# A two-layer graph network on one core: loads in order of use, and two slots of the main loop in another order

## The chip, the cores and the metric

The kernel runs on one core of a Trainium2 chip. The core has five engines that work side by side and wait for each other through semaphores: TensorE (matrix products, and the loading of weights for them), VectorE, ScalarE, GpSimd and SyncE (which issues most of the transfers). The metric is the device time of one execution in microseconds (us), as the median of several runs. In the profile TensorE's products are PE and its weight loads PEld, VectorE is DVE, ScalarE is ACT, GpSimd is POOL, and the queue of SyncE is SPq.

## What is computed

`x` is 64 graphs of 256 nodes with 512 features in float32; `adj` is one 256 x 256 matrix of zeros and ones that all of them share. Layer 0 is a graph convolution, layer 1 an attention of 8 heads under the mask of `adj`. After each, the input is added and the rows are normalized.

```python
# layer 0
Wi, Wj = W[:, :512], W[:, 512:]
mi, mj = x @ Wi.T, x @ Wj.T                       # per graph: 256x512 @ 512x512
out = deg[:, None] * (mi + b) + a @ mj            # a = adj as float, deg = its row sums
x = layernorm(x + out)
# layer 1
q, k, v = (split_heads(x @ W.T + b) for W, b in ((Wq, bq), (Wk, bk), (Wv, bv)))   # 8 heads of 64
scores = where(adj == 0, -inf, q @ k.T / 8)
out = merge_heads(softmax(scores) @ v) @ Wo.T + bo
x = layernorm(x + out)
```

## The kernel before

Every 512 x 512 product is made of seven products of half blocks in place of eight, Strassen's scheme in Winograd's form: sums of blocks of the left operand (`S1` to `S4`, made on VectorE) meet sums of blocks of the weights (`T1` to `T4`, made once). The kernel's list of layer-0 steps for one graph `b` is this (steps 1 to 7 are the seven products, each of four records on TensorE; `bank` gives one of three PSUM banks, `score_banks` one of two pairs of banks):

```python
def left_steps(f, order=anywhere):
    return [lambda: order(nc.vector.tensor_add(f["S1"], f["A21"], f["A22"])),   # L477
            lambda: order(nc.vector.tensor_sub(f["S2"], f["S1"], f["A11"])),   # L478
            lambda: order(nc.vector.tensor_sub(f["S3"], f["A11"], f["A21"])),  # L479
            lambda: order(nc.vector.tensor_sub(f["S4"], f["A12"], f["S2"]))]   # L480
# ... (cut)
    def split(t):
        nc.scalar.copy(k["hi"][:, t, :], k["mj"][:, t, :])                      # L524
        nc.gpsimd.tensor_tensor(k["lo"][:, t, :], k["mj"][:, t, :],             # L525
                                k["hi"][:, t, :].bitcast(F32), ALU.subtract)

    def step1():
        product("x", raw(0, 0), B11, True)
        nc.scalar.copy(keeper("u1"), banks["x"])
    def step2():
        product("w", raw(1, 1), T4, True)
        add_scaled(1, banks["w"])
    def step3():
        product("x", raw(0, 1), B21, False)
        add_scaled(0, banks["x"])
    def step4():
        product("y", xS[b]["S2"], T2, True)
        nc.vector.tensor_add(keeper("u2"), banks["y"], k["u1"])
    def step5():
        product("z", xS[b]["S1"], T1, True)
        k["mj"] = p1.tile([P, NT, D], F32, tag="mj", name="mj")
        nc.scalar.copy(k["mj"][:, 1, :], banks["z"])                            # L547
    def step6():
        product("y", xS[b]["S3"], T3, False)
        nc.vector.tensor_add(keeper("u3"), banks["y"], k["u1"])                 # L551
        nc.gpsimd.tensor_tensor(k["mj"][:, 1, :], k["mj"][:, 1, :], k["u3"], ALU.add)   # L552
        # ... (cut: tiles for hi and lo)
        split(1)
        add_scaled(1, k["u3"])                                                  # L520
    def step7():
        product("z", xS[b]["S4"], B22, False)
        nc.vector.tensor_add(k["mj"][:, 0, :], banks["z"], k["u2"])             # L561
        split(0)

    def neighbours():                       # the graph's product, a @ mj, in two parts of mj
        k["pa"] = score_banks("pa")
        for i in (1, 0):
            for n, (j, part) in enumerate((j, part) for j in (1, 0) for part in ("hi", "lo")):
                matmul(k["pa"][:, i, :], graph[:, j, i * P:(i + 1) * P], k[part][:, j, :],
                       start=(n == 0), stop=(n == 2 * NT - 1))
    def take(t):                            # adds pa to xh, statistics of the normalization
    def give(t):                            # normalizes; send_h writes the result out, turned
    return [step1, step2, step3, step4, step5, step6, step7, neighbours, lambda: take(1), lambda: take(0),
            lambda: give(1), lambda: send_h(b, 1), lambda: give(0), lambda: send_h(b, 0)]
```

Attention goes by units `w` of two heads of one graph. `scores` starts the score products and returns the rest, which adds the mask on VectorE, takes the exponential on ScalarE and adds up on GpSimd:

```python
def scores(g, w):
    ps = score_banks("ps").rearrange("p j (t q) -> p j t q", t=NT)
    # ... (cut: eight score matmuls into ps)
    def exponentials():
        pe = p2.tile([P, 2, NT, N], F32, tag="pe", name="pe")
        nc.vector.tensor_add(pe, ps, maskT)                                     # L805, operands cut
        in_order(nc.scalar.activation(flat, flat, AF.Exp, scale=QSCALE, ...))   # L809
        nc.gpsimd.tensor_tensor(pk, pe[:, :, 0, :], pe[:, :, 1, :], ALU.add)    # L812
    return exponentials
```

The main loop makes 31 passes. In each, the attention of two graphs is mixed with layer 0 of the next two (`p` and `q` are their lists of steps), slot by slot:

```python
def layer0(g):
    p, q = l0_steps(b1), l0_steps(b2)
    return [p[:3] + [item(turn_x, b2)] + p[3:4],
            p[4:7] + [item(sum_x, b2), item(add_bias, b2)] + q[:1],
            p[7:10], p[10:] + q[1:3],
            q[3:6] + [item(turn_h, b1)] + q[6:7],
            q[7:], [item(turn_h, b2)]]
# ... (cut)
for g in range(NG - 1):
    # ... (cut)
    run(work[0])
    for w in range(2, NB * NC, 2):          # w = 2, 4, 6: the second, third and fourth slot
        values(g, w - 2)                    # products with v, into pav
        values(g, w - 1)
        multiply()                          # aoT times the spread inverses of the slot before, GpSimd (L844)
        divide_two(g, w - 1)                # den on TensorE, reciprocal on VectorE (L887), spread by transfers
        scores(g, w)()
        if w == 4:
            run(work[2])
        later = scores(g, w + 1)
        later()
        run(work[w // 2 if w < 4 else w // 2 + 1])
```

`turn_x(b)` transposes the loaded `x` on VectorE (L485), `sum_x(b)` makes its four sums (`xS`), `add_bias(b)` adds the bias times the degrees to `xh` on GpSimd (L374). In the opening, `make_factors` makes `T1` to `T4` of an attention weight with four VectorE subtractions and writes them to memory, and `check_graph` makes the mask with three VectorE operations.

Of the kernel before, what the change touches and what calls it, by code (L numbers as in the profile page):

```python
# [8 lines left out]
F32 = mybir.dt.float32  # L9
# [7 lines left out]
P = 128  # L17
# [207 lines left out]
def unshifted_path(ctx, tc, flag, x, adj, wiT, wjT, b0, wqT, bq, wkT, bk, wvT, bv, woT, bo, out):  # L225
# [72 lines left out]
    def load_x(b):  # L298
        if b < B:
            xh[b] = p6.tile([P, NT, D], F32, tag="xh", name="xh")  # L300
            nc.sync.dma_start(out=xh[b], in_=x[b].rearrange("(t p) d -> p t d", p=P))
# [1 line left out]
    b_bc = p4.tile([P, D], F32, tag="u", name="b_bc")  # L303
    xB, hB = {}, {}

    def load_xB(b):
        if b < B:
            xB[b] = p1.tile([P, N // R, P], F32, tag="xB", name="xB")
            for q in range(D // P):
                nc.sync.dma_start(out=xB[b][q * R:(q + 1) * R],  # L310
                                  in_=x[b][:, q * P:(q + 1) * P].rearrange("(r a) n -> r a n", r=R))
# [1 line left out]
    load_xB(0)  # L313
    w0 = const.tile([P, 7, 2, D], F32, name="w0")
    adj_i = p2.tile([P, NT, N], I32, tag="pe", name="adj_i")
    for n, w, h in ((B11, wiT, 0), (T3, wjT, 0), (None, None, 0), (B21, wiT, 1), (B22, wjT, 1)):
        if n is None:
            nc.sync.dma_start(out=adj_i, in_=adj.rearrange("(t p) j -> p t j", p=P))
        else:
            nc.sync.dma_start(out=w0[:, n], in_=w.rearrange("(p h c) o -> p h c o", h=2, c=2)[:, h])  # L320
    load_x(0)
    nc.sync.dma_start(out=b_bc, in_=b0.to_broadcast([P, D]))

    xT, xS, hT, hS, qT, kT, vv, aoT, oS = ({} for _ in range(9))
# [44 lines left out]
    def degree_bias():  # L369
        for t in range(NT):  # L370
            in_order(nc.vector.tensor_scalar(degb[:, t, :], b_bc, deg[:, t:t + 1], None, ALU.mult))
# [116 lines left out]
    def turn_x(b, tag="xT"):  # L488
        if b < B:
            xT[b] = p1.tile([P, NC, N], F32, tag=tag, name="xT")  # L490
            transposed(xT[b], xB.pop(b))
            load_xB(b + 1)

    def sum_x(b):
        if b < B:
# [6 lines left out]
    def l0_steps(b):  # L502
        banks, k = {}, {}

        def product(name, left, n, first):
            if first:
                banks[name] = bank("po")
            for c in range(2):
                matmul(banks[name], left[:, c, :], w0[:, n, c, :], start=(first and c == 0),
                                 stop=(c == 1), skip_group_check=True)  # L510

        def raw(t, h):
            return xT[b][:, 2 * h:2 * h + 2, t * P:(t + 1) * P]

        def keeper(name):
            k[name] = p3.tile([P, D], F32, tag="lu", name=name)
            return k[name]

        def add_scaled(t, src):
            nc.vector.scalar_tensor_tensor(xh[b][:, t, :], src, deg[:, t:t + 1], xh[b][:, t, :],  # L520
                                           ALU.mult, ALU.add)

        def split(t):
            nc.scalar.copy(k["hi"][:, t, :], k["mj"][:, t, :])  # L524
            nc.gpsimd.tensor_tensor(k["lo"][:, t, :], k["mj"][:, t, :], k["hi"][:, t, :].bitcast(F32),  # L525
                                    ALU.subtract)
# [14 lines that stand above are left out]
            product("y", xS[b]["S2"], T2, True)  # L541
            nc.vector.tensor_add(keeper("u2"), banks["y"], k["u1"])

        def step5():
            product("z", xS[b]["S1"], T1, True)
            k["mj"] = p1.tile([P, NT, D], F32, tag="mj", name="mj")
            nc.scalar.copy(k["mj"][:, 1, :], banks["z"])  # L547

        def step6():
            product("y", xS[b]["S3"], T3, False)  # L550
            nc.vector.tensor_add(keeper("u3"), banks["y"], k["u1"])  # L551
            nc.gpsimd.tensor_tensor(k["mj"][:, 1, :], k["mj"][:, 1, :], k["u3"], ALU.add)  # L552

            k["hi"] = p1.tile([P, NT, D], F32R, tag="hi", name="hi")
            k["lo"] = p1.tile([P, NT, D], F32R, tag="lo", name="lo")
            split(1)
            add_scaled(1, k["u3"])

        def step7():
# [4 lines that stand above are left out]
        stats = {}  # L564

        def neighbours():
# [6 lines that stand above are left out]
        def take(t):  # L573
            r = xh[b][:, t, :]
            in_order(nc.vector.tensor_add(r, k["pa"][:, t, :], r))
            stats[t] = norm_stats(r, in_order)

        def give(t):
            norm_apply(xh[b][:, t, :], *stats[t], in_order)


        return [step1, step2, step3, step4, step5, step6, step7, neighbours, lambda: take(1), lambda: take(0),
                lambda: give(1), lambda: send_h(b, 1), lambda: give(0), lambda: send_h(b, 0)]

# [315 lines left out]
    def layer0(g):  # L900

        b1, b2 = NB * g, NB * g + 1

        def item(f, *args):
            return lambda: f(*args)

        p, q = l0_steps(b1), l0_steps(b2)
        return [p[:3] + [item(turn_x, b2)] + p[3:4],
                p[4:7] + [item(sum_x, b2), item(add_bias, b2)] + q[:1],
                p[7:10], p[10:] + q[1:3],  # L910
                q[3:6] + [item(turn_h, b1)] + q[6:7],
                q[7:], [item(turn_h, b2)]]

    def run(steps):
        for s in steps:
            s()

    def with_output_bias(g, k):
        return [*k[:2], lambda: add_output_bias(NB * g), k[2], lambda: add_output_bias(NB * g + 1), *k[3:]]
# [8 lines left out]
    def combine(n, m, k):  # L928
        in_order(nc.vector.tensor_sub(w0[:, n], w0[:, m], w0[:, k]))
# [11 lines left out]
    combine(T2, B22, T1)  # L941
    combine(T4, B21, T2)
    combine(T3, B22, T3)
    p, q = l0_steps(0), l0_steps(1)
    run([p[0], p[2], p[4], p[3]])
    turn_x(1, "hB")
    degree_bias()
    add_bias(0)
    turn_graph()
    run([p[1], p[5], q[0], p[6], q[2]])  # L950
# [22 lines left out]
    h_transpose(1, 1)  # L973
    h_transpose(1, 0)
    run(o[2:])
    check_graph()
    run(with_output_bias(0, k)[2:])
    run(v[2:3])
    turn_x(2)
    sum_x(2)  # L980
    add_bias(2)
    run(v[3:5])
    make_factors(woT, "wo", raw_o)
    load_x(3)
    run([scores(0, 0), scores(0, 1)])
    run(v[5:])
    for g in range(NG - 1):
        load_x(NB * (g + 2))
        load_x(NB * (g + 2) + 1)
        work = layer0(g + 1)  # L990
        run(work[0])
        for w in range(2, NB * NC, 2):
            values(g, w - 2)
            values(g, w - 1)
            multiply()
            divide_two(g, w - 1)
            scores(g, w)()
            if w == 4:
                run(work[2])
            later = scores(g, w + 1)  # L1000
            later()
            run(work[w // 2 if w < 4 else w // 2 + 1])
        w = NB * NC - 2
        values(g, w)
        values(g, w + 1)
        multiply()
        o = o_steps(g)
        q = second_late(qk_steps(g + 1, qT, "qT", bq_sb, bqd))
        k = second_late(qk_steps(g + 1, kT, "kT", bk_sb, bkd, True))
        v = second_late(v_steps(g + 1, True))  # L1010
        neighbours, take1, take0, give1, send1, give0, send0 = work[SLOTS + 1]
        inverses = divide_at_once(g, w + 1, lambda: run([o[0], neighbours, take1, take0]))
        run([q[0], give1, send1, o[1], give0, send0, *left_steps(oS[g], in_order), k[0], q[1], k[1]])
        end_values(inverses)
        run(o[2:6] + work[SLOTS + 2] + [v[0], o[6], v[1]])
        end = finish_steps(g)
        k = with_output_bias(g + 1, k)[2:]
        run(q[2:5] + end[:1] + q[5:6] + end[1:2] + q[6:7] + end[2:3] + k[:1] + end[3:4] + k[1:] + end[4:] + v[2:3])
        turn_x(NB * (g + 2))
        sum_x(NB * (g + 2))  # L1020
        if g + 2 < NG:
            add_bias(NB * (g + 2))
        run(v[3:5])
        run([scores(g + 1, 0), scores(g + 1, 1)])
        run(v[5:])
# [93 lines left out]
```

## Time and profile before

| | |
|---|---|
| time, median of 3 runs | 3117.78 us (3116.93 to 3118.83) |
| span of the profiled execution | 3115.8 us |
| VectorE busy | 2227.6 us, 71% |
| GpSimd busy | 1504.5 us, 48% |
| ScalarE busy | 998.4 us, 32% |
| transfers | 439.13 MB, 141 GB/s on average |
| mean granted clock of TensorE | 0.999 |

A row of a timeline reads: start in us from the span's beginning, duration in us, engine, source line, operation, output and inputs by name, shape, count of instructions that were merged; in square brackets the idle time of the engine ahead of it and what ended it. A busy share is an average over the whole span. An engine that is idle elsewhere can still be the one that is waited for in one slot, so the rows of the slots matter more here than the shares.

### The profile page before, as it was taken

The numbers are of one execution on the slowest core, as the hardware profiler recorded it, in microseconds if no ns is written. First come the engines' busy times: TensorE is split into PE (matmuls) and PEld (weight loads), VectorE is DVE, ScalarE is ACT, GpSimd is POOL, SyncE is SP. The second block draws the span as 40 slices with busy tenths as digits, with TensorE's granted clock in tenths as the row PEclk, the third lists the DMA queues.
The fourth block names the chain that finished last, engine by engine and source line by source line (L and its number), as shares of the span: only waits on it lengthen the run. The fifth ranks groups of instructions, "written<-read, shape, count | busy, mean of one in ns | idle before, by whom it ended". The sixth has DMA issues, their size and how long they took to land. (4 is left out here: it accounts for less than half of the span.)

```text
span 3115.8 us, 42525 instructions
## 1 busy us (share of the span) xinstructions
PE 3082.4 (99%) x14598; PEld 2131.7 (68%) x14598; DVE 2227.6 (71%) x3327; ACT 998.4 (32%) x1894; POOL 1504.5 (48%) x1255
## 2 busy tenths in 40 slices
PE   8999999999999999999999999999999999999998
PEld 4667766677766777666776667776677766677665
DVE  6777777776777767776777777677776777767775
ACT  2332333323333333333233332333333333323332
POOL 2544445544545445454454544454544546445453
PEclk9999999999999999999999999999999999999999
DMA  7345534455444554445553445544455444555332
GB/s 252 118 146 153 162 116 131 129 154 160 139 119 125 152 164 144 117 129 149 154 162 113 132 132 153 162 134 121 125 152 166 142 117 127 151 157 159 111 112 93
DMA packets 398490, 439.13 MB, mean 141 GB/s; under 512 B 36928, under 2 KB 288320, under 8 KB 397888
## 3 DMA queue, kind: packets, MB, share of 16 engines
q1 hardware_dynamic: 398272, 436.36, 46.7%
q8 instruction: 120, 1.97, 0.3%
q14 instruction: 98, 0.80, 0.1%
HBM read 340.79 MB, written 70.25 MB: 132 GB/s over the span
## 5 line engine op out<-in xcount | busy, mean ns | idle before, releaser
L461 POOL TENSOR_TENSOR rstd<-ve,mhalf 128x1 f32<-128x1 f32 x256 | 140.4, 552 | 717.7 <-DVE below L459 717.7
L812 POOL TENSOR_TENSOR pk<-pe 128x512 f32<-128x512 f32 x256 | 322.1, 1274 | 336.4 <-ACT pe L809 336.2
L290 PE MATMUL po<-w,xS 128*128 128x512 f32 x1024 | 471.7, 603 | 6.1 <-ACT mj L547 5.7
L290 PE MATMUL st<-hS,factor 128*128 128x256 f32 x2048 | 452.7, 379 | 1.2 <-DVE u L685 1.2
L290 PEld LDWEIGHTS st<-hS,factor 128*128 128x128 f32 x2048 | 388.4, 190 | 55.1 <-DVE u L685 1.6
L809 ACT ACTIVATE pe<-pe 128x1024 f32<-128x1024 f32 x256 | 270.8, 1058 | 379.2 <-DVE pe L805 379.2
L290 PE MATMUL po<-w,xT 128*128 128x512 f32 x768 | 354.0, 603 | 12.9 <-DVE xT L485 10.9
L290 PEld LDWEIGHTS po<-w,xS 128*128 128x128 f32 x1024 | 187.5, 190 | 253.5 <-issue 192.6
L290 PE MATMUL st<-hT,factor 128*128 128x256 f32 x1536 | 360.1, 381 | 0.7 <-ACT hT L622 0.7
L290 PEld LDWEIGHTS st<-hT,factor 128*128 128x128 f32 x1536 | 289.0, 190 | 52.4 <-ACT u L711 11.8
L805 DVE TENSOR_TENSOR pe<-ps,maskT 128x1024 f32<-128x1024 f32 x256 | 297.9, 1194 | 32.9 <-PE ps L290 32.9
L290 PEld LDWEIGHTS po<-w,xT 128*128 128x128 f32 x768 | 144.1, 191 | 181.0 <-issue 163.3
L290 PE MATMUL ps<-qT,kT 64*128 64x256 f32 x2048 | 264.9, 392 | 0.0
L290 PE MATMUL pav<-pe,v_sb 128*64 128x256 f32 x2048 | 250.1, 386 | 1.9 <-ACT pe L809 1.8
L740 DVE TENSOR_TENSOR xh<-st,xh 128x512 f32<-128x512 f32 x186 | 142.9, 768 | 138.1 <-PE st L290 138.1
L290 PEld LDWEIGHTS pav<-pe,v_sb 128*64 128x64 f32 x2048 | 135.2, 136 | 154.2 <-issue 71.9
L290 PEld LDWEIGHTS ps<-qT,kT 64*128 64x128 f32 x2048 | 184.3, 186 | 78.2 <-issue 51.3
L290 PE MATMUL st<-factor,hS 128*128 128x256 f32 x1024 | 234.8, 382 | 0.0
L888 POOL TENSOR_TENSOR rtot<-rtot,rden 128x256 f32<-128x256 f32 x96 | 70.0, 729 | 332.2 <-DVE rden L887 332.2
L290 PE MATMUL st<-factor,oS 128*128 128x256 f32 x992 | 224.2, 379 | 0.0
L887 DVE RECIPROCAL rden<-den 128x256 f32<-128x256 f32 x96 | 168.4, 1754 | 71.6 <-PE den L290 70.0
L290 PEld LDWEIGHTS st<-factor,hS 128*128 128x128 f32 x1024 | 191.9, 190 | 35.4 <-issue 10.6
(115 smaller groups left out, 4808.1 us busy)
## 6 DMA issues: line engine op xcount, KB each, us to landing
xB<-in_x_dram SPq DMA_DIRECT2D x256, 128.0 KB, 3.6
xh<-in_x_dram SPq DMA_DIRECT2D x64, 512.0 KB, 4.1
factor<-wq SPq DMA_DIRECT2D x128, 256.0 KB, 3.6
factor<-wk SPq DMA_DIRECT2D x128, 256.0 KB, 2.6
factor<-wv SPq DMA_DIRECT2D x128, 256.0 KB, 2.6
factor<-wo SPq DMA_DIRECT2D x124, 256.0 KB, 2.9
h_cols<-xh SPq DMA_DIRECT2D x124, 256.0 KB, 2.4
hB<-h_cols SPq DMA_DIRECT2D x62, 512.0 KB, 3.6
```

What stands on the lines that cost most here:

```text
L290: in_order(nc.tensor.matmul(*args, **kw))
L461: nc.gpsimd.tensor_tensor(rstd, ve, mhalf, ALU.pow)
L740: nc.vector.tensor_add(dst, src, dst)
L805: nc.vector.tensor_add(pe.rearrange("p j t q -> p j (t q)"), ps.rearrange("p j t q -> p j (t q)"), maskT.rearrange("p t q -> p (t q)").uns ...
L809: in_order(nc.scalar.activation(flat, flat, AF.Exp, scale=QSCALE, accum_out=etot[:, NB * g + i, pr:pr + 1]))
L812: nc.gpsimd.tensor_tensor(pk, pe[:, :, 0, :], pe[:, :, 1, :], ALU.add)
L887: nc.vector.reciprocal(rden, den)
L888: nc.gpsimd.tensor_tensor(rtot, rtot, rden, ALU.add)
```

## The change

It has four parts. In the opening, the weights' loads stand in the order in which they are used and the first goes through ScalarE's queue, and the second `x` is loaded early into a buffer of its own and transposed earlier. Further on in the opening, the factors of `wo` are made earlier and the graph's check later. In the second slot the products come as step 6, step 5, the next graph's step 1, step 7, so that more work lies between step 5 and step 7, which share a bank; `join` lets step 5 and 6 come in either order. In the third slot both groups of scores come together, then a product of the next graph, then the graph's product, then another product.

```diff
-    def load_xB(b):
+    def load_xB(b, tag="xB"):
...
-    for n, w, h in ((B11, wiT, 0), (T3, wjT, 0), (None, None, 0), (B21, wiT, 1), (B22, wjT, 1)):
-        if n is None:
-            nc.sync.dma_start(out=adj_i, in_=adj.rearrange("(t p) j -> p t j", p=P))
-        else:
-            nc.sync.dma_start(out=w0[:, n], in_=w.rearrange("(p h c) o -> p h c o", h=2, c=2)[:, h])
+    for queue, n, w, h in ((nc.scalar, B11, wiT, 0), (nc.sync, B21, wiT, 1), (nc.sync, T3, wjT, 0), (nc.sync, B22, wjT, 1)):
+        queue.dma_start(out=w0[:, n], in_=w.rearrange("(p h c) o -> p h c o", h=2, c=2)[:, h])
+    nc.sync.dma_start(out=adj_i, in_=adj.rearrange("(t p) j -> p t j", p=P))
     load_x(0)
+    load_xB(1, "hS")
...
-            load_xB(b + 1)
+            if b > 0:
+                load_xB(b + 1)
...
+        def join(*needed):
+            if all(n in k for n in needed):
+                nc.gpsimd.tensor_tensor(k["mj"][:, 1, :], k["mj"][:, 1, :], k["u3"], ALU.add)
+                k["hi"] = p1.tile([P, NT, D], F32R, tag="hi", name="hi")
+                k["lo"] = p1.tile([P, NT, D], F32R, tag="lo", name="lo")
+                split(1)
...
-                p[4:7] + [item(sum_x, b2), item(add_bias, b2)] + q[:1],
-                p[7:10], p[10:] + q[1:3],
+                [p[5], p[4], q[0], p[6], item(sum_x, b2), item(add_bias, b2)],
+                q[1:2] + p[7:10] + q[2:3] + p[10:],
...
+    turn_x(1, "hB")
+    degree_bias()
     p, q = l0_steps(0), l0_steps(1)
     run([p[0], p[2], p[4], p[3]])
-    turn_x(1, "hB")
-    degree_bias()
...
     run(o[2:])
+    make_factors(woT, "wo", raw_o)
+    run(with_output_bias(0, k)[2:])
     check_graph()
-    run(with_output_bias(0, k)[2:])
...
-    make_factors(woT, "wo", raw_o)
...
-            scores(g, w)()
-            if w == 4:
-                run(work[2])
-            later = scores(g, w + 1)
-            later()
-            run(work[w // 2 if w < 4 else w // 2 + 1])
+            run([scores(g, w), scores(g, w + 1)] + work[w // 2])
```

`run` calls its items one after another. In the last line `scores(g, w)` and `scores(g, w + 1)` are called while the list is made, so both groups of score products come first, and then the two `exponentials`.

More of the change, by code (lines that the diff above doesn't have):

```diff
@@ L304, in unshifted_path @@
     xB, hB = {}, {}
-    def load_xB(b):
+    def load_xB(b, tag="xB"):
         if b < B:
-            xB[b] = p1.tile([P, N // R, P], F32, tag="xB", name="xB")
+            xB[b] = p1.tile([P, N // R, P], F32, tag=tag, name="xB")
             for q in range(D // P):
@@ L547, in step5 @@
             nc.scalar.copy(k["mj"][:, 1, :], banks["z"])
+            join("u3")
         def step6():
@@ L551, in step6 @@
             nc.vector.tensor_add(keeper("u3"), banks["y"], k["u1"])
[L552 to L556, printed above, removed]
+            join("mj")
             add_scaled(1, k["u3"])
@@ L1010, in unshifted_path @@
         v = second_late(v_steps(g + 1, True))
-        neighbours, take1, take0, give1, send1, give0, send0 = work[SLOTS + 1]
+        neighbours, take1, take0, give1, send1, give0, send0 = work[SLOTS]
         inverses = divide_at_once(g, w + 1, lambda: run([o[0], neighbours, take1, take0]))
@@ L1014, in unshifted_path @@
         end_values(inverses)
-        run(o[2:6] + work[SLOTS + 2] + [v[0], o[6], v[1]])
+        run(o[2:6] + work[SLOTS + 1] + [v[0], o[6], v[1]])
         end = finish_steps(g)
```

## Prediction

> **What bounds the kernel now.** I read the page's busy shares first, then the timeline of TensorE alone over one pass of the main loop, then VectorE and GpSimd over the same stretch, then the opening. The page:
>
> ```profile
> PE 3082.4 (99%) x14598; PEld 2131.7 (68%) x14598; DVE 2227.6 (71%) x3327; ACT 998.4 (32%) x1894; POOL 1504.5 (48%) x1255
> ```
>
> TensorE sets the end; anything gained must be one of its gaps, and there are few. One pass of the loop (31 in all) goes from 188.23 to 284.17, 95.94 us, by the starts of two equal groups of score matmuls; 31 x 95.94 = 2974 of the 3116 us. The second and third slot of that pass on TensorE:
>
> ```profile
> 205.05 3.70 PE L290 MATMUL po<-w,xS 128*128 128x512 f32 x8
> 208.93 1.98 PE L290 MATMUL po<-w,xS 128*128 128x512 f32 x4 [0.18 <-ACT mj L547]
> 210.75 1.88 PE L290 MATMUL po<-w,xT 128*128 128x512 f32 x4
> ...
> 215.01 1.13 PE L290 MATMUL ps<-qT,kT 64*128 64x256 f32 x8
> 216.07 0.50 PE L290 MATMUL pa<-hi,graph 128*128 128x512 f32 x1
> ...
> 218.13 1.13 PE L290 MATMUL ps<-qT,kT 64*128 64x256 f32 x8
> 219.19 3.70 PE L290 MATMUL po<-w,xT 128*128 128x512 f32 x8
> 222.82 1.95 PE L290 MATMUL pav<-pe,v_sb 128*64 128x256 f32 x16
> ```
>
> A layer-0 product is four records of 0.43 us, 1.72 us. Two full products from 205.05 (and 0.10 for the change of shape ahead of them) would end at 208.58; the third starts at 208.93, so step 7 waits 0.35 us for ScalarE's copy of `z`. Scores and graph product take 219.19 - 215.01 = 4.18 us with the graph between the score groups.
>
> VectorE, then GpSimd, from the same two slots:
>
> ```profile
> 210.95 0.69 DVE L561 TENSOR_TENSOR mj<-po,u 128x512 f32<-128x512 f32 x1 [0.55 <-PE po L290]
> 211.56 0.42 DVE L477 TENSOR_TENSOR xS<-xT 128x256 f32<-128x256 f32 x1
> 212.01 0.43 DVE L478 TENSOR_TENSOR xS<-xS,xT 128x256 f32<-128x256 f32 x1
> 212.35 1.50 DVE L479 TENSOR_TENSOR xS<-xT 128x256 f32<-128x256 f32 x1
> 213.78 1.50 DVE L480 TENSOR_TENSOR xS<-xT,xS 128x256 f32<-128x256 f32 x1
> 215.20 1.75 DVE L887 RECIPROCAL rden<-den 128x256 f32<-128x256 f32 x1
> 216.86 1.16 DVE L805 TENSOR_TENSOR pe<-ps,maskT 128x1024 f32<-128x1024 f32 x1
> ```
>
> ```profile
> 209.82 1.71 POOL L552 TENSOR_TENSOR mj<-mj,u 128x512 f32<-128x512 f32 x1
> 212.26 2.73 POOL L525 TENSOR_TENSOR lo<-mj,hi 128x512 fp32r<-128x512 f32 x2 [0.73 <-ACT hi L524]
> 214.95 2.57 POOL L374 TENSOR_TENSOR xh<-xh,degb 128x1024 f32<-128x1024 f32 x1
> 217.47 1.30 POOL L844 TENSOR_TENSOR aoT<-aoT,spread 128x512 f32<-128x512 f32 x1
> ```
>
> See that the same `xS` sum takes 0.42 us when GpSimd is idle and 1.50 when a `lo` runs: it ends some 0.3 us after that `lo`. VectorE first, then the waiting GpSimd operation, then VectorE again: they alternate.
>
> The opening, timeline of TensorE and then busy time by stretch (columns: PE, PEld, DVE, ACT, POOL, granted clock, DMA share, GB/s):
>
> ```profile
> 27.15 3.17 PE L290 MATMUL po<-w,xT 128*128 128x512 f32 x4 [2.78 <-DVE xT L485]
> ```
>
> ```profile
> 17.50:27.80 10.30, 7.52 (x21) 3.27 (x20) 4.72 (x6) 1.20 (x2) 1.82 (x2) 1.00 1.00 379
> 27.80:31.20 3.40, 3.40 (x6) 1.32 (x5) 1.68 (x3) 1.28 (x3) 3.04 (x2) 0.50 1.01 393
> ```
>
> TensorE idles 2.78 us for the second transposed `x`, and the following 3.4 us run at half clock.
>
> **What the Trainium skill says.** "SBUF — State Buffer", section "Who interferes with whom": a VectorE instruction with two SBUF inputs and a GpSimd one that reads SBUF exclude each other for the whole instruction. The trace agrees (0.42 against 1.50 us), and shows that VectorE's PSUM readers (`mj`, `pe`, reciprocal) are not held. "TensorE: Matmul & The Clock Gate", Part 1: a free-running window of 3413 ns, half clock after an idle window. The 3.4 us at 0.50 after a window with 2.78 us idle agree. "Trainium Kernel Development and Optimization", "Key Constraints": queues share the 16 DMA engines, another queue saves only issue time; so the first weight's move to ScalarE's queue should give little, and TensorE's start (8.15) hangs on the first transposition (6.04 to 8.10) anyway.
>
> **The change part by part.**
>
> *Second slot.* Step 7 now comes a product later: order step 6, step 5, the next batch's step 1, step 7. The wait of 0.35 us and the 0.10 for the restart go: 0.45 us a pass. TensorE: step 6 from 205.04 to 206.86, step 5 to 208.57, step 1 to 210.29, step 7 to 212.01. Step 5's copy can run from 208.78 (0.2 us after the product, as in the rows above `mj` follows its product) to 209.35, before 210.29: the wait really goes.
>
> *Third slot.* Both score groups, then one product, the graph's eight, the other product. Each switch between 64-row scores and the graph's matmuls costs about 0.10 us on each side (the first graph record is followed after 0.34 us, the others after 0.23); product and graph join without it. By group times: before 1.06 + 2.06 + 1.06 + 3.63 = 7.81; after 1.93 (sixteen score records together, as from 203.12 to 205.05) + 1.82 (1.72 and a switch) + 1.86 (8 x 0.232) + 1.81 = 7.42. Gain 0.40 us a pass.
>
> Together 0.85 x 31 = 26 us, if nothing new is waited for. But something is:
>
> *VectorE in the third slot.* Score banks are two. The graph's product used to take the free one; now both score groups stand in them, and the graph's waits for the first `pe` addition. VectorE's order ahead of that is fixed: `mj`, four `xS` sums, reciprocal, `pe`. `mj` needs step 7, which ends at 212.01 instead of 210.75. I shift the rows by hand:
> - GpSimd: `mj` addition to 211.5 and the first `lo` 212.24 to 213.5 as before (ScalarE's copy is no later than GpSimd's `pk`).
> - VectorE: `mj` 212.21 to 212.90. First sum: behind the first `lo`, ends 213.8.
> - Second `lo` is ready at 213.6 (its cast 0.70 us earlier, at 212.9), so it goes first: to 214.9. Second sum ends 215.2.
> - The 2.35 us bias addition (2.57 in the row, with its own wait) is next: 215.06 to 217.4. Third sum ends 217.7.
> - `aoT` multiplication: to 218.85. Fourth sum ends 219.1.
> - Reciprocal (1.75) 219.05 to 220.8, `pe` (1.16) to 221.9.
>
> TensorE: pav and den (2.45) after step 7 and its switch to 214.55, scores to 216.48, one product to 218.30. The graph's matmuls could start at 218.3 and get their bank at 221.9: a wait of 3.6 us, with 0.1 for the restart. Net per pass: 3.7 - 0.85 = +2.9 us; x 31 = +90 us.
>
> *Clock.* A gap of 3.6 us meets a 3.41 us window at any phase. A window with as much idle as the opening's (2.78) occurs for offsets over 1.5 us of 3.41, 44% of passes, more if less idle is enough. A half-clock window costs at most 1.7 us of TensorE's work. Estimate from these: 0.7 us a pass, 22 us.
>
> *Opening.* Second `x` has its own buffer and is transposed ahead of `u3`: after `u2` (21.30) and one graph copy (0.41), 2.07 us, so at 23.8, before TensorE comes to it at 24.4. That removes 2.78 us and the half-clock window (1.7). Against it: `wo`'s four differences (two SBUF inputs each) now stand among the two output-bias additions (75.87 to 80.96) before the `u` that TensorE waits for at 81.9; I reckon 1.4 us more there. Net -3 us.
>
> Sum: 3117.8 + 90 + 22 - 3 = 3227.
>
> **The rivals.**
> - *The gaps close and no new wait matters* (-26 - 3): 3089. For it: the old wait and the switches are plain, and VectorE is 71% busy over the span. Against it: VectorE is busy 8.08 of the 8.40 us from 214.4 to 222.8 (busy time by stretch), no slack where the new dependence lies. About one in six.
> - *A milder lock order*: if the second sum slips in ahead of the second `lo` (0.2 us decide), all four sums end one GpSimd operation earlier, at about 218.0, and the wait is 2.5 us: +1.75 x 31 = 54, with some half-clock 3180. One in five.
> - *The clock drops in every pass*: 31 x 1.5 on top of the 90 instead of 22: 3250.
> - *The later graph product delays the next slot*: `hB` would land near 236.2 and is wanted at 237.0 by VectorE; slack of 0.8 us, so I add nothing, but it could add a few tenths a pass.
>
> **Range and chances.** Three of the five outcomes lie between 3180 and 3260; I take 3222, a little under the sum for the milder cases, and 3120 to 3265 as the range, which leaves the first rival outside. The 2% line is 3180: slower by over 2% 0.72, within 2% 0.27, faster by over 2% 0.01.
>
> **What would show it.** Right: among TensorE's waits a new row, `pa` from VectorE's `pe`, some 31 times at about 3.6 us; the last three `xS` sums of the second slot at 1.4 to 2.6 us each; the reciprocal of the third slot about 4 us later than the den it reads; a granted clock under 0.999; step 7's wait for the `mj` copy gone; no 2.78 us gap near 24. Wrong: `pa` following the product at once, or the first `pe` addition done before that product ends; then the lock order above fails and the first rival holds.

## The result and the profile after

| | before | after |
|---|---|---|
| time, median | 3117.41 us (3116.93 to 3118.83) | 3223.89 us (3218.76 to 3226.18) |
| ratio | | 1.0339, 95% interval 1.0321 to 1.0356 |
| span of the profiled execution | 3115.8 us | 3220.1 us |
| one pass of the main loop | 95.99 us | 98.93 us in 22 passes, 100.2 to 101.8 us in 9 |
| mean granted clock of TensorE | 0.999 | 0.993 |

The changed kernel is 3.4% slower; 3222 with a range of 3120 to 3265 had been predicted. The first line of the page after:

```profile
PE 3081.3 (96%) x14598; PEld 2145.8 (67%) x14598; DVE 2322.4 (72%) x3327; ACT 1006.9 (31%) x1894; POOL 1507.4 (47%) x1255
```

TensorE is busy as long as before to 1 us (3082.4), and its share falls from 99% to 96%: its idle time has grown by 105 us. That the busy times agree is chance: run 5 below, with the same products in the same order and no half clock in the loop, has 3059.7 us, so the half clock takes back about what the two new orders save. TensorE's waits after, as engine, line and operand that waited, what it waited for, us in total, times, longest:

```profile
PE pa L290 <- DVE pe L811: 110.1, 31, 3.6
PE po L290 <- DVE xT L485: 9.9, 1, 9.9
PE st L290 <- DVE u L691: 2.7, 1, 2.7
```

The first row is new: the graph's product (`pa`) waits in each of the 31 passes for VectorE's mask addition `pe`, 3.55 us each. The 31 waits of step 7 for the copy of `z`, of which the same view of the kernel before has this row, are gone:

```profile
PE po L290 <- ACT mj L547: 5.7, 31, 0.2
```

The other two rows of the view after belong to the opening.

The timeline of VectorE after, from the second slot into the third (the rows that answer to those of before, some 2 us later because the clock and the pass have moved):

```profile
213.80 0.69 DVE L567 TENSOR_TENSOR mj<-po,u 128x512 f32<-128x512 f32 x1 [3.04 <-PE po L290]
214.40 0.99 DVE L477 TENSOR_TENSOR xS<-xT 128x256 f32<-128x256 f32 x1
215.43 1.38 DVE L478 TENSOR_TENSOR xS<-xS,xT 128x256 f32<-128x256 f32 x1
216.74 2.57 DVE L479 TENSOR_TENSOR xS<-xT 128x256 f32<-128x256 f32 x1
219.23 1.48 DVE L480 TENSOR_TENSOR xS<-xT,xS 128x256 f32<-128x256 f32 x1
220.63 1.74 DVE L893 RECIPROCAL rden<-den 128x256 f32<-128x256 f32 x1
222.30 2.28 DVE L811 TENSOR_TENSOR pe<-ps,maskT 128x1024 f32<-128x1024 f32 x2
```

And GpSimd's over the same stretch:

```profile
213.83 2.70 POOL L526 TENSOR_TENSOR lo<-mj,hi 128x512 fp32r<-128x512 f32 x2 [0.73 <-ACT hi L525]
216.49 2.54 POOL L374 TENSOR_TENSOR xh<-xh,degb 128x1024 f32<-128x1024 f32 x1
218.98 1.44 POOL L850 TENSOR_TENSOR aoT<-aoT,spread 128x512 f32<-128x512 f32 x1
```

Read the two side by side. Every sum ends just after one GpSimd operation. The row of `lo` holds two operations, which end at 215.11 and 216.53; the first sum ends at 215.39 and the second at 216.81. The third ends at 216.74 + 2.57 = 219.31, the bias addition at 219.03; the fourth at 220.71, the `aoT` multiplication at 220.42. Four operations that take 0.42 us each when nothing is in their way (1.7 us together) take 6.3 us from 214.40 to 220.71. "SBUF — State Buffer", section "Who interferes with whom", is the note of the Trainium skill that describes this exclusion; the 2.57 us row is a wait inside an instruction and not a cost of the sum. The busy share counts it all the same: VectorE's busy time rises from 2227.6 to 2322.4 us with the same 3327 instructions.

What TensorE does meanwhile:

```profile
218.06 1.98 PE L290 MATMUL po<-w,xT 128*128 128x512 f32 x4
223.60 0.47 PE L290 MATMUL pa<-hi,graph 128*128 128x512 f32 x1 [3.56 <-DVE pe L811]
```

The product of the next graph ends near 220.0, and the graph's product starts when the first of the two `pe` has left its bank, near 223.5 (222.30 plus half of 2.28).

The two spans differ by 104.3 us. By the pass starts: opening -2.7, 31 passes +107.5, end -0.5. Of the 107.5, 31 x (98.93 - 95.99) = 91.1 is the wait less the two gains; the other 16.4 lies almost wholly in the nine passes with half-clock windows. (In every trace here the granted clock changes only at edges a whole number of 3.413 us apart: after, the half clock of the start ends at 13.38, and the first one in the loop goes from 122.61 to 126.02, 32 and 33 such stretches later. A "window" below is one stretch between two edges.)

### The profile page after: what moved, and what is told of

It reads as the page before. It is cut to its first block, busy times and chain, and to the rows that moved or that the text cites. A ratio compares the mean times of both kernels' runs of the same rounds, so it can differ in the third digit from the quotient of the medians.

```text
span 3220.1 us, 42525 instructions
## 1 busy us (share of the span) xinstructions
PE 3081.3 (96%) x14598; PEld 2145.8 (67%) x14598; DVE 2322.4 (72%) x3327; ACT 1006.9 (31%) x1894; POOL 1507.4 (47%) x1255
## 5 line engine op out<-in xcount | busy, mean ns | idle before, releaser
L818 POOL TENSOR_TENSOR pk<-pe 128x512 f32<-128x512 f32 x256 | 334.7, 1328 | 324.8 <-ACT pe L815 324.7
L290 PE MATMUL ps<-qT,kT 64*128 64x256 f32 x2048 | 256.5, 389 | 0.0
L290 PE MATMUL pa<-hi,graph 128*128 128x512 f32 x256 | 117.9, 461 | 110.1 <-DVE pe L811 110.1
```

Of the source, the lines that this page charges most:

```text
L290: in_order(nc.tensor.matmul(*args, **kw))
```

## The experiments

All times are medians; the kernel before had 3117.4 to 3117.75 us beside them.

**1. The second slot's order alone.** Kernel before, with `join` and

```diff
-                p[4:7] + [item(sum_x, b2), item(add_bias, b2)] + q[:1],
+                [p[5], p[4], q[0], p[6], item(sum_x, b2), item(add_bias, b2)],
```

> The kernel before with the second slot's new order alone; third slot and opening as before. Theory A (step 7 a product later puts VectorE's sums behind GpSimd's lo, bias addition and aoT multiplication; the reciprocal and the first pe addition follow 3.8 us later): the wait stays and only moves to the second score group, which needs the bank that the first pe addition frees. It would be ready at 214.55 + 1.06 + 2.06 = 217.7 and get its bank at 221.9: 4.2 us, net of the 0.45 gained 3.8 us x 31 = +117, with some half-clock windows 3240 to 3280. Rival B (it is the third slot's grouping, which fills both pairs of score banks): no wait without the grouping, 3117 - 14 = 3103.

Measured: 3313.58 us (3313.09 to 3315.99), ratio 1.0631 (1.0615 to 1.0647), clock 0.968. Its wait:

```profile
PE ps L290 <- DVE pe L810: 130.5, 31, 4.2
```

The mechanism needs no new third slot: later sums alone make the reciprocal and `pe` late, and then it is the second group of scores that waits for a bank, 4.2 us as expected. The time was missed by some 34 us above the upper end of the theory's range, because the clock is worse than thought. From the third pass on every pass is 102.40 us long with 6.83 us at half clock. 102.40 is 30 x 3.413, thirty windows of the clock: a gap that falls in two windows in one pass does so in the next as well. Without the clock the sum would be 3117.4 + 31 x (4.2 + 0.1 - 0.45) = 3237; the remaining 77 us are 2.5 us a pass.

**2. The third slot's order alone.** Kernel before, with both groups of scores first and

```diff
-                p[7:10], p[10:] + q[1:3],
+                q[1:2] + p[7:10] + q[2:3] + p[10:],
```

> The kernel before with the third slot's new order alone; second slot and opening as before. Theory A: the sums end at 215.3 as before, the first pe addition at 218.0, the graph's product is ready at 212.6 + 2.45 + 1.93 + 1.82 = 218.8: no wait, and the 0.40 us a pass of the saved switches stay: 3117 - 12 = 3105. Rival B (the grouping is what costs): the graph's product waits for its bank here too, about 3.5 us x 31, over 3200.

Measured: 3106.35 us (3104.35 to 3106.55), ratio 0.9961 (0.9947 to 0.9974). No wait for `pa`; a typical pass takes 95.59 us, 0.40 under before, the switches saved. So the third slot's order is a gain as long as the sums come as early as they did. The loss needs the second slot's order, and is there without the third's.

**3. The bias addition late.** Changed kernel, with one GpSimd operation taken from among the four that the sums meet:

```diff
-                [p[5], p[4], q[0], p[6], item(sum_x, b2), item(add_bias, b2)],
-                q[1:2] + p[7:10] + q[2:3] + p[10:],
+                [p[5], p[4], q[0], p[6], item(sum_x, b2)],
+                q[1:2] + p[7:10] + [item(add_bias, b2)] + q[2:3] + p[10:],
```

> The changed kernel with the second graph's bias addition on GpSimd (2.35 us) moved from the second slot to after the graph's take in the third; all else the same, VectorE's work too. Theory A (the sums wait for GpSimd's operations one by one): one of the three operations they queue behind is gone, so the third sum ends 2.1 us earlier, the reciprocal runs about 216.9 to 218.6, pe to 219.8 against 218.3 when the graph's product is ready; the wait falls from 3.55 to about 1.5 us and the half-clock windows go: 3224 - 64 - 20 = 3140. Rival C (VectorE simply has too much work there, whatever GpSimd does): nothing changes, 3224.

Measured: 3166.7 us (3165.32 to 3166.89), ratio 1.0157 (1.0142 to 1.0173); no half-clock window in the loop. TensorE's waits:

```profile
PE pa L290 <- DVE pe L811: 43.4, 31, 1.4
PE po L290 <- DVE u L543: 18.2, 31, 0.6
```

The wait for `pa` is 1.4 us, as expected of theory A; the total is 27 us over it. The second row was not expected: where the bias addition went, it holds up VectorE's next reader of `xh`, and `pe` and `u` behind that. VectorE's timeline of this kernel:

```profile
227.25 0.75 DVE L521 SCALAR_TENSOR_TENSOR xh<-po,deg,xh 128x512 f32<-128x512 f32 x1 [0.66 <-POOL xh L374]
```

**4. The sums late.** Changed kernel, with `sum_x` after the graph's product:

```diff
-                [p[5], p[4], q[0], p[6], item(sum_x, b2), item(add_bias, b2)],
-                q[1:2] + p[7:10] + q[2:3] + p[10:],
+                [p[5], p[4], q[0], p[6], item(add_bias, b2)],
+                q[1:2] + p[7:10] + [item(sum_x, b2)] + q[2:3] + p[10:],
```

> The changed kernel with the four sums of the second graph moved from the end of the second slot to after the graph's take in the third. Theory A: VectorE goes from mj (212.9) to the reciprocal (214.65) and the first pe addition ends at 217.5, before the graph's product is ready at 218.3: no wait. The 0.85 us a pass stay, less perhaps 0.3 where the next slot's first product waits for a sum behind GpSimd: 3117 - 26 - 3 = 3088, or up to 3098. Rival B (banks): a wait of 3.5 us remains, over 3200. Rival C (VectorE too full): the work only moves, and the wait comes back in the fourth slot, 3150 or more.

Measured: 3126.36 us (3124.67 to 3127.87), ratio 1.0027 (1.0017 to 1.0038). The wait for `pa` is gone altogether, with all of the change's orders on TensorE in place. But the sums are now on the way of the fourth slot:

```profile
PE po L290 <- DVE xS L478: 15.0, 31, 0.5
PE po L290 <- DVE u L543: 11.6, 31, 0.4
```

A pass is 96.35 us, 1.2 above the 95.14 (95.99 less 0.85) that theory A stands for. Neither theory held in its number: A is right that the sums make the wait, and wrong that they can be put there for nothing.

**5. The sums early, in a buffer of their own.** What keeps the second graph's sums behind step 7 is that both graphs share one `xS` buffer, which step 7 reads last. Changed kernel with

```diff
-                                p1.tile([P, 4, 2, P], F32, tag="xS", name="xS"))
+                                p1.tile([P, 4, 2, P], F32, tag=f"xS{b % NB}", name="xS"))
...
-                [p[5], p[4], q[0], p[6], item(sum_x, b2), item(add_bias, b2)],
+                [p[5], p[4], q[0], item(sum_x, b2), p[6], item(add_bias, b2)],
```

> The changed kernel, but the second graph's sums have an xS buffer of their own, so they no longer wait for the last reader of the first graph's sums, and stand ahead of step 7, where VectorE had 3.0 us of idle time (210.8 to 213.8). All the work of the changed kernel is there, only the queue behind GpSimd is left. Theory A (the wait for pa is the sums' alternation with GpSimd, nothing else): S1, S2 at 0.42 us each, one sum held by the 1.3 us mj addition, the reciprocal follows its den at once (216.4 to 218.1), the first pe ends near 219.2, the third slot's product at 220.0; no wait for pa, no half-clock window, nothing pushed into the fourth slot: before less 26 less 2.7 = 3088 to 3092 us. Rival D (the third slot's order itself costs, because the graph's product must wait for pe in whatever order the sums stand, or the fourth slot takes new waits as in the runs with the bias or the sums moved late): 3110 to 3160 us.

Measured: 3090.34 us (3087.76 to 3091.28), ratio 0.9913 (0.99 to 0.9926), clock 0.999. VectorE's timeline:

```profile
207.36 1.49 DVE L477 TENSOR_TENSOR xS<-xT 128x256 f32<-128x256 f32 x1
208.88 1.37 DVE L478 TENSOR_TENSOR xS<-xS,xT 128x256 f32<-128x256 f32 x1
210.18 0.41 DVE L479 TENSOR_TENSOR xS<-xT 128x256 f32<-128x256 f32 x1
210.51 0.41 DVE L480 TENSOR_TENSOR xS<-xT,xS 128x256 f32<-128x256 f32 x1
210.85 0.68 DVE L567 TENSOR_TENSOR mj<-po,u 128x512 f32<-128x512 f32 x1
212.95 1.76 DVE L893 RECIPROCAL rden<-den 128x256 f32<-128x256 f32 x1 [1.42 <-PE den L290]
```

TensorE's over the same product and the graph's:

```profile
214.74 1.98 PE L290 MATMUL po<-w,xT 128*128 128x512 f32 x4
216.16 0.80 PE L290 MATMUL pa<-hi,graph 128*128 128x512 f32 x1
```

GpSimd's, over the first two sums:

```profile
205.61 2.96 POOL L818 TENSOR_TENSOR pk<-pe 128x512 f32<-128x512 f32 x2 [1.46 <-ACT pe L815]
208.53 1.45 POOL L547 TENSOR_TENSOR mj<-mj,u 128x512 f32<-128x512 f32 x1
```

Two sums still wait for GpSimd, but now in VectorE's idle time: the second behind the `mj` addition (1.37 us), as was expected of one, and the first behind a `pk` addition (1.49 us where 0.42 was expected). The reciprocal waits for `den` again and not for VectorE, and the graph's product joins the one before it. A typical pass is 95.14 us, 0.85 under before: both predicted gains in full. All the work of the changed kernel is there, in the same order on TensorE, ScalarE and GpSimd; only VectorE's order and the buffer differ. This shows that the place of the sums behind step 7, and nothing else of the two slots' new orders, cost the time. This version beats both kernels.

**6. The bias addition early.** As run 3, but the addition goes to the first slot, where GpSimd has nothing to do:

```diff
-        return [p[:3] + [item(turn_x, b2)] + p[3:4],
-                [p[5], p[4], q[0], p[6], item(sum_x, b2), item(add_bias, b2)],
+        return [p[:2] + [item(add_bias, b2)] + p[2:3] + [item(turn_x, b2)] + p[3:4],
+                [p[5], p[4], q[0], p[6], item(sum_x, b2)],
```

> The changed kernel, but the bias addition of the second graph (2.54 us on GpSimd) stands in the first slot, where GpSimd is idle for 9.5 us, in place of late in the third slot's list as in the run with the bias late. Theory A: the sums lose one of the four GpSimd operations they queue behind, fourth sum ends 218.4 in place of 220.7, so the wait for pa falls from 3.55 to 1.3-1.4 us and the half-clock windows go; and as nothing is moved into the fourth slot, its new waits (0.6 us each for u) are not there: 3224 less 31 x 2.2 less 17 = 3137 to 3142 us. Rival (the fourth slot's waits come from the third slot's shape and not from the late bias): about 3167 as in the run with the bias late.

Measured: 3139.74 us (3137.97 to 3141.05, without one execution of 3667.78 us whose granted clock was 0.817), ratio 1.0072 (1.0059 to 1.0085), clock 0.999.

```profile
PE pa L290 <- DVE pe L811: 43.3, 31, 1.4
```

The same 1.4 us as in run 3, and no wait for `u`: the 27 us that run 3 had over its expectation came from the place to which the addition had gone. Taking away one of the four GpSimd operations takes 2.15 us off the wait, close to the 2.35 to 2.54 us that this operation lasts.

**7. The second buffer, with the first weight's load behind the first `x`.** As run 5, and

```diff
-    for queue, n, w, h in ((nc.scalar, B11, wiT, 0), (nc.sync, B21, wiT, 1), ...
+    for queue, n, w, h in ((nc.sync, B11, wiT, 0), (nc.sync, B21, wiT, 1), ...
```

> As the run with the second buffer, and the first weight's load goes through SyncE's queue again, behind the first x, as before the change. Theory A (the load on ScalarE's queue took bandwidth from the first x, so its transposition and TensorE's start came 1.8 us late): TensorE starts near 8.2 instead of 9.9 us, time 1.8 us under the run with the second buffer. Rival (the start is late because of the order of loads, not the queue, or the time is lost again at the second or third product, which then waits for its weight): no difference.

Measured: 3089.24 us (3088.36 to 3090.01), ratio 0.9912 (0.9899 to 0.9925): 1.1 us under run 5, with intervals that overlap, so no difference is shown. TensorE's first product:

```profile
8.95 3.68 PE L290 MATMUL po<-w,xT 128*128 128x512 f32 x4 [8.95 <-DMA w<-in_wiT_dram]
```

The first transposition starts at 5.99 us as before the change (7.84 in the changed kernel, 8.28 in run 5), so the load on ScalarE's queue did delay the first `x`. The four loads of that `x` are issued from 0.74 us on in both runs and take 3.1 us (median) to landing in run 7, 5.3 in run 5; their first packet starts at 2.28 us in run 7 and at 3.27 in run 5, where the weight's packets run from 1.76 to 4.58. So about 1.0 us of the delay is a later start, after the weight's first packets; what the rest is was not traced. But then TensorE waits for the weight itself, until 8.95, so the start is 0.7 to 1.4 us sooner than with two queues and not 1.8. The theory is right that this load delays the first `x`; that it does so by taking bandwidth is not shown. The rival is right that part of the gain is lost again to a weight.

**8. The opening alone.** Kernel before with all the edits of the opening, and both slots in the old order (the diff is the opening's part of the change's).

> The kernel before with the opening of the change alone (loads, second x in its own buffer, earlier transposition, factors of wo and graph's check swapped); both slots in the old order. Theory A: the loop is untouched (95.99 us a pass), the opening gives 2.7 us: 3115 us, ratio 0.9991. Rival: the opening is worth nothing or less by itself, because the later start (1.8 us) outweighs what is saved: 3118 or more.

Measured: 3116.23 us (3113.99 to 3116.94), ratio 0.9995 (0.9987 to 1.0003): the interval holds 1, so 1.5 us of gain are not shown. Its passes take 95.99 us, as before. Why the value is uncertain is seen from the profiles' openings (start of the first product, end of the half clock that the kernel starts with, start of the first pass; us):

| kernel | opening | first product | full clock from | first pass |
|---|---|---|---|---|
| before | old | 8.15 | 17.57 | 90.73 |
| run 2 | old | 8.52 | 17.37 | 90.82 |
| run 1 | old | 8.30 | 11.67 | 88.92 |
| run 5 | new | 10.39 | 18.48 | 90.38 |
| run 6 | new | 9.65 | 18.57 | 90.05 |
| run 8 | new | 9.63 | 18.46 | 89.98 |
| after | new | 9.94 | 13.38 | 88.04 |
| run 3 | new | 10.26 | 13.97 | 88.47 |
| run 4 | new | 9.71 | 13.11 | 87.80 |
| run 7 | new, one queue | 8.95 | 12.43 | 87.82 |

The full clock came early where a window of the clock fell whole into the first product, which takes about 3.7 us (after: it begins at 9.94, the window is 13.38 - 3.41 = 9.97 to 13.38), and about 5 us later where the first window was partly idle and the next one held the 0.7 us gap before the second product (run 8: windows from 8.22, 11.63 and 15.05, the gap at 13.4). Part 1 of "TensorE: Matmul & The Clock Gate" says that the window runs free and doesn't start with the kernel; these ten openings agree. Compared at like clock, the new opening with the load on ScalarE's queue reaches the first pass 0.35 to 0.85 us sooner (late clock: runs 5, 6 and 8 against before and run 2) or 0.45 to 1.1 us sooner (early clock: after, runs 3 and 4 against run 1). Most of the 2.7 us between the profiles of before and after is the window's phase.

## Why the prediction was right

*The new wait.* Right in place, cause and size. Counted from the start of `mj`, the fourth sum was to end after 6.89 us and ended after 6.91; the reciprocal after 8.59 and 8.57; the first `pe` after 9.69 and about 9.65. Each sum stood behind the very GpSimd operation that the prediction named. The wait was put at 3.6 us and is 3.55. Runs 5 and 6 show the cause by taking it away whole and in part.

*The two gains of 0.45 and 0.40 us a pass.* Right, and hidden in the result. Run 2 shows 0.40 for the third slot; run 5 shows 0.85 for both.

*Net loss a pass.* +2.9 predicted, +2.94 measured. The parts are less exact: 3.55 - 0.85 + 0.1 makes 2.80. The 0.14 above it is in time that the profile counts as busy. From the start of the product to the second record of the graph's product it is 223.91 - 218.06 = 5.85 us in the changed kernel and 216.80 - 214.74 = 2.06 in run 5, where nothing waits: 3.79 us are lost, and 3.79 - 0.85 is 2.94. In run 6 the same stretch is 3.69 us, 1.63 over run 5, and its pass of 96.79 is 1.65 over. So the idle time in a row understates what the wait costs, here by 0.24 us; before the change, step 7's row showed 0.18 us where 0.35 was lost.

*The clock.* 22 us predicted, 16.4 measured; 9 of 31 passes have half-clock windows, not 44%. Two steps failed, and the number came out near by luck, because they work against each other. The first is how much idle time brings the half clock: the 2.78 us of the opening were taken. When TensorE's idle time is counted window by window in all ten traces, from the start of the full clock on, the clock fell after 53 full-clock windows, which had 2.00 to 3.41 us of idle time, and after none with 1.99 us or less (two with 2.01 us passed). A gap of 3.55 us then passes only where two windows share it at 1.55 to 2.0 us each, 0.45 of 3.41 us; at any phase some 27 of 31 passes would have lost the clock (an estimate from these numbers). The second is that the gap meets the window at any phase. The undisturbed pass of 98.93 us is 0.05 us short of 29 windows (98.98), so the phase hardly moves: the window in which the gap begins holds 1.77, 1.83, 1.89, 1.93 and 1.99 us of it in passes 13 to 17. The trace has a stretch of twelve undisturbed passes, and cold ones in clusters. Run 1, at 30 windows a pass, is the same thing on its bad side.

*The opening.* -3 predicted; the profiles give -2.7, but that agreement is luck. The step "TensorE's start (8.15) hangs on the first transposition anyway" forgot that the transposition hangs on the first `x`, which the weight's load on ScalarE's queue delays: the start is 1.8 us later. The removal of the 2.78 us gap (1.0 us for `u` stands in its place) and of the half-clock window at 27.8 is there, and so are the 1.5 us more at `u` (2.7 against 1.2; 1.4 was reckoned). With 2.78 - 1.0 + 1.7 for what is removed and 1.8 + 1.5 for what is added, 0.2 us are left; the comparison at like clock gives 0.35 to 1.1.

*The rivals.* No new wait (3089): run 5 is that outcome, 3090, once the sums are out of the way. The milder lock order did not occur; the second sum stood behind the second `lo`. A drop of the clock in every pass did not occur in the changed kernel, but in run 1. The delay of the next slot by a later `hB` did not occur: VectorE waits for `hB` 0.6 us in the whole span.

## What to carry to other kernels

An engine that is idle elsewhere can be the limit of one slot; before work is moved later on TensorE, follow what its consumer does next, instruction by instruction, to the next thing TensorE needs. Where VectorE sums with both inputs in SBUF meet GpSimd's work, as here, count each short sum at the length of the GpSimd operation it will stand behind, and look for a place where GpSimd is idle or VectorE is; here a second 4 KB-per-partition buffer turned +3.4% into -0.9%. Compare openings only at the same phase of the clock.

## What was not expected of the hardware

- A loop can lock onto the clock's window. With a gap of 4.2 us, run 1 settled at 102.40 us a pass, 30 x 3.413, with two half-clock windows in each of its last 29 passes; with a gap of 3.55 us, the changed kernel ran at nearly 29 windows and lost the full clock for one or two windows in 9 of 31 passes. That the pass settles because the length and the phase fix each other is read from the traces and was not tested. Gaps of 1.4 us a pass (runs 3 and 6) cost no clock at all.
- In these traces the half clock came after windows with about 2.0 us or more of idle time out of 3.41, so a gap of 2.77 us costs it in one window (run 2, at 24.4 us) and not when it is split into 1.08 and 1.63 us over two (run 5, 2.71 us at 78.8 us).
- A load issued at once through another engine's queue delayed the load that mattered by 1.1 to 2.3 us: the transposition of the first `x` started at 5.99 to 6.41 us without it (before and runs 1, 2 and 7) and at 7.51 to 8.28 us with it (after and runs 3, 4, 5, 6 and 8).
